# The first image's small key maps in another buffer, and softmax sums inverted in transposed form, in a three-stage attention and expert kernel

## The chip, the cores and the metric

The kernel runs on one core of one Trainium2 chip, as one launch. The metric is the device time of that launch in microseconds (us), the median of three runs. All data are float32.

## What is computed

The input is a batch of 8 images of 256 channels by 32 x 32 pixels. Layer 0 normalises them, attends with pooled keys and values and adds the result back; layer 1 is a self-attention over the 1024 pixels and then a gated mixture of 8 experts. Cut to what the change touches, layer 0 is:

```python
q = einsum('bchw,oc->bohw', x, q_w)                 # 8 heads of 32
k_map, v_map = split(einsum('bchw,oc->bohw', x, kv_w))
def pooled(t):
    outs = []
    for i, r in enumerate([1, 2, 3, 6]):            # maps of 32x32, 16x16, 11x11, 5x5
        p = average_pool(t, r)
        p = p + depthwise_3x3(p, dconv_w[i], dconv_b[i])
        outs.append(p.reshape(B, C, -1))
    return concatenate(outs, axis=2)                # 1426 keys
k, v = layernorm(pooled(k_map)), layernorm(pooled(v_map))
out = softmax(q @ k.T * SCALE) @ v
x = x + proj(mix(out))
```

## The kernel before, in words

**Stages.** Layer 0 and layer 1's attention are woven into one stretch; the experts follow. The last result of layer 0's attention leaves PSUM at 1856.7 us in the profile, the first expert matmul starts at 1893.2 us. What can still be late at the end is TensorE's expert work alone.

**Layer 0's attention** (`attention`, from line 913; main loop from line 1892). Each of the 8 images is worked in 4 units: two groups of four heads (`c`) by two halves of the 1024 pixels. A unit has 11 steps, one for each 128 keys (`kc`); the first unit of an image has one more, `kc` 11, which makes the tail of 18 keys for all four units and is placed ninth, after `kc` 7 (`order`, line 1892). A step makes scores on TensorE (`sc`), takes their exponential on ScalarE into a `pt` buffer of 128 x 2048 (six of them), and one step later multiplies by the values on TensorE (`pv`). The tail's exponentials go to a buffer of their own, `ptail`, of 128 x 4 x 512. There is one PSUM buffer for the scores, so each `sc` waits for the exponential before it.

**Sums.** The `pt` buffers of two steps are added by a DMA that GpSimd's queue issues (`add`, line 1564), and these pairs by VectorE (`sums`, line 1571). A TensorE product with ones gives the sum of each softmax row, 32 equal rows for each head. ScalarE copies this from PSUM to `rec` and in passing records a bound (`hi`); `normalise` (line 1590) inverts `rec` on VectorE, multiplies the unit's output by it, and ScalarE reads `rec` once more for the other bound (`lo`). If a bound is passed, a second, general program runs at the end; it doesn't in this case.

**Keys and values.** A thread projects each image to four maps of 1426 columns (`m` 0 and 1 keys, 2 and 3 values) on TensorE; ScalarE copies each to `p` and writes the middle tap into `acc`. The 3 x 3 convolution is then eight multiply-adds on VectorE for each of the four levels of a map (`taps`, line 1243). For the first image alone, the keys' large level is convolved on TensorE instead (`first_keys`, line 1220), and the keys' `p` lies in two of the six `pt` buffers (`first_maps`, line 1172); their `acc` are the buffers `kn` and `v`. `first_taps` (line 1257) does the values' large level, and then the three small levels of maps 2, 3, 0, 1 in that order. The keys of 1024 to 1425 can be finished once `whole` holds 0 and 1 (`key_tokens`), the values of these columns once it holds 2 and 3 (`value_tokens`).

**What orders the work.** The program is straight-line code for each engine. `Flow` (line 657) writes it: generators (threads) with ranks offer their next instruction, and a table of costs (`cost`, line 723) keeps a planned time for each engine and tile, by which `step` chooses the next thread. Between two steps of the main loop TensorE gets filler work: the projections of the next image, layer 1's weights (`weights1`), layer 1's attention. Everything that a thread issues between two `yield`s is put into the queues as it stands. Every engine then runs its queue in order. `f.finish` in the main loop holds back the next step until a condition is met, and issues what is needed for it first: line 1909 for the keys, line 1921 for the tail, and these lines for the two borrowed buffers:

```python
if i == 4:
    f.finish(lambda: {0, 1}.issubset(whole))
```

All instructions issued through `Flow` carry line 670 in the profile, so its lines are told apart by the names of the tiles.

Of the kernel before, what the change touches and what calls it, by code (L numbers as in the profile page):

```python
# [10 lines left out]
AF = mybir.ActivationFunctionType  # L11
# [5 lines left out]
P = 128  # L17
C = 256
HW = 1024
# [893 lines left out]
def attention(tc, kit, f, outer, ended, nb, consts, x, t1, t2, hn, bounds, vecs, q_t, kv_t, proj_t, gqk_t, wqk, wqkv, vecs1, w1_d, w1c, gate_d, wrc, vecs2, bnvec):  # L913
# [6 lines left out]
    with ExitStack() as ctx:  # L920
# [5 lines left out]
        def T(pool, shape, tag, bufs=1):  # L926
            return f.tile(pool, shape, tag, bufs=bufs)
# [153 lines left out]

        ks, qs, vts = {}, {}, {}
        ptail = T(work, [P, 4, 512], "ptail")
        vz = [T(work, [P, P], f"vz{i}") for i in range(2)]
        for t in vz:
            f.pool.memset(t, 0.0)
# [7 lines left out]
        def ve(*tiles):  # L1094
            return "DVE", tiles, None
# [76 lines left out]
        def first_maps(xp):  # L1172


            for m in range(4):
                if m < 2:
                    p = T(work, [P, 4, 512], "pt", bufs=6).rearrange("p j q -> p (j q)")
                    acc = T(l1, [P, NK], "v") if m else T(work, [P, NK], "kn", bufs=3)
                else:
                    p = pmaps[m - 2]  # L1180
                    acc = T(work, [P, NK], "acc", bufs=3)
                for t in (p, acc):
                    if t is not p or m < 2:
                        f.split(t, 512, HW)
                first[m] = p, acc
            for m, s0 in [(m, s0) for g in (0, 2) for s0 in (0, 512) for m in (g, g + 1)] + [(m, HW) for m in range(4)]:
                if s0 == HW:
                    yield until(lambda: pooled)
                w = min(512, NK - s0)
                c = m % 2  # L1190
                p, acc = first[m]
                src = source(xp, s0, w)
                yield pe(src, tag="sm")
                ps = small()
                for k in range(2):
                    f.pe.matmul(
                        ps[:, :w],
                        lhsT=kvw[:, k, m * P : (m + 1) * P],
                        rhs=src[:, k, :],
                        start=k == 0,  # L1200
                        stop=k == 1,
                    )
                f.act.activation(p[:, s0 : s0 + w], ps[:, :w], AF.Copy)
                for s, n in enumerate(SIDES):
                    a, z = max(OFFS[s], s0), min(OFFS[s] + n * n, s0 + w)
                    if a < z and (m >= 2 or s):
                        f.act.activation(
                            acc[:, a:z],
                            ps[:, a - s0 : z - s0],
                            AF.Identity,  # L1210
                            bias=db(c, s),
                            scale=mid[:, c * 4 + s : c * 4 + s + 1],
                        )
                if (m, s0) == (3, 512):
                    large.append("maps")
                    f.spawn(first_keys(0), 1)
                    f.spawn(first_keys(1), 5)
            whole.append("maps")
# [21 lines left out]
                f.act.activation(acc[:, half * 512 : half * 512 + 512], ps, AF.Identity, bias=db(m, 0))  # L1240
            large.append(("keys", half))

        def taps(c, s, p, acc):
            n, o = SIDES[s], OFFS[s]
            pin = p[:, o : o + n * n].rearrange("p (h w) -> p h w", h=n)
            pout = acc[:, o : o + n * n].rearrange("p (h w) -> p h w", h=n)
            for tap in range(9):
                if tap == 4:
                    continue
                dy, dx, y0, y1, x0, x1 = windows(tap, n)  # L1250
                o_ap = pout[:, y0:y1, x0:x1]
                yield ve(pin[:, y0 + dy : y1 + dy, x0 + dx : x1 + dx], o_ap)
                f.ve.scalar_tensor_tensor(
                    o_ap, pin[:, y0 + dy : y1 + dy, x0 + dx : x1 + dx], dw(c, s, tap), o_ap, ALU.mult, ALU.add
                )

        def first_taps():
            for m in (2, 3):
                yield until(lambda: "maps" in large)
                yield from taps(m - 2, 0, *first[m])  # L1260
                large.append(("values", m))
                read[0] += 1
            yield until(lambda: whole)
            for m in (2, 3, 0, 1):
                for s in range(1, 4):
                    yield from taps(m % 2, s, *first[m])
                whole.append(m)
            done.extend(first[m][1] for m in (2, 3, 0, 1))

# [301 lines left out]
        def sums(n, pairs):  # L1571

            for i in range(1, NKC // 2):
                yield until(lambda: len(pairs) > i)
                for j in range(0, 4, 2):
                    s = pairs[0][:, j : j + 2, :]
                    yield ve(s, pairs[i])
                    f.ve.tensor_tensor(s, s, pairs[i][:, j : j + 2, :], ALU.add)
            yield until(lambda: normalised[0] == n)
            yield pe(pairs[0], tag="sm")  # L1580
            total = small()
            for j in range(4):
                f.pe.matmul(
                    total[DH * j : DH * j + DH, :], lhsT=kit.ones[:, :DH], rhs=pairs[0][:, j, :], start=True, stop=True
                )
            rec = T(work, [P, 512], "rec")
            f.act.activation(rec, total, AF.Copy, accum_out=hi[:, column[n] : column[n] + 1])
            return rec

        def normalise(b, c, sl, rec, n):  # L1590
            att = atts[b, c][:, sl]
            yield ve(rec)
            f.ve.reciprocal(rec, rec)
            f.ve.tensor_tensor(att, att, rec, ALU.mult)
            yield act(rec)
            f.act.activation(rec, rec, AF.Copy, accum_out=lo[:, column[n] : column[n] + 1])
# [276 lines left out]
        mt = T(wp, [P, 2, C], "mt")  # L1873
        bias = T(wp, [P, 2], "mtb")
        def unit(b, c, sl, n, pairs):
            rec = yield from sums(n, pairs)
            yield from normalise(b, c, sl, rec, n)
            normalised[0] += 1
            if c and sl.start:
                f.spawn(project(b), 1)  # L1880
# [23 lines left out]
        for i in range(len(steps) + 1):  # L1904
            if i < len(steps):
                b, c, half, kc = steps[i]
                sl = slice(half * 512, half * 512 + 512)
                if kc % 4 == 0:
                    f.finish(lambda: key_parts[0] > 3 * b + kc // 4)
                if (half, kc) == (0, 0):  # L1910
                    f.finish(lambda: (b, c) in qs and (b or (c, 0) in asked))
                    turn[0] = 2 * b + c
                    atts[b, c] = T(work, [P, HW], "att", bufs=2)
                if kc == NKC // 2 and b < nb - 1:
                    f.sp.dma_start(t1[b][:, c, sl], x[b, c * P : (c + 1) * P, sl])
                if i == 4:
                    f.finish(lambda: {0, 1}.issubset(whole))
                if b == 0 and kc == 0:
                    f.finish(lambda: (c, half) in asked)
                if kc == NKC - 1:  # L1920
                    f.finish(lambda: key_parts[0] > 3 * b + 2 and (b, 1) in qs and (b or len(asked) == 4))
                    tail_scores(b)
                else:
                    pts[i] = scores(b, c, sl, kc)
                f.step()
            if i and steps[i - 1][3] < NKC - 1:
                b1, c1, half1, kc1 = steps[i - 1]
                if kc1 == 0:
                    pv = T(psum, [P, 512], "pv")
                    pairs = []  # L1930
                    sl1 = slice(half1 * 512, half1 * 512 + 512)
                    f.spawn(unit(b1, c1, sl1, units, pairs), 0)
                    units += 1
                f.finish(lambda: kc1 // 4 in vts[b1])
                values(b1, c1, kc1, pts[i - 1], pv)
                if kc1 % 2:
                    add(kc1, pts.pop(i - 1), pts[i - 2])
                    pairs.append(pts.pop(i - 2))
                if kc1 == NKC - 2:
                    u = 2 * c1 + half1  # L1940
                    tail_values(b1, u, pv)
                    pairs.append(pts.pop(i - 1))
                    tail_add(u, pairs[-1])
                    f.finish(lambda: projected[0] >= b1)
                    f.act.activation(atts[b1, c1][:, sl1], pv, AF.Copy)
            if i < len(steps):
                f.step((PACE, PACE1))
# [687 lines left out]
```

## Time and profile before

| what | value |
|---|---|
| runs | 3240.96, 3236.12, 3240.89 us; median 3240.89 us |
| profiled execution | 3236.82 us, of which the span of the instructions is 3235.0 us |
| TensorE busy | 3064.9 us (95%) |
| VectorE busy | 2458.7 us (76%) |
| ScalarE busy | 1692.2 us (52%) |
| GpSimd busy | 1198.6 us (37%) |
| 80.88 to 1860.12 us: TensorE, VectorE, ScalarE busy | 1650.55, 1434.52, 1154.57 of 1779.24 us |
| inversion of a unit's sums on VectorE | 32 times 3.35 us |

The profile is of one execution. In its lines PE is TensorE, PEld its weight load, DVE VectorE, ACT ScalarE, POOL GpSimd, SP SyncE; `out<-in` names what is written and read. In a timeline line the first number is the start in us, the second the length, and the bracket tells how long the engine stood idle before and what ended that.

### The profile page before, as it was taken

Reading aid. Unit: us, or ns where it says so; the run is one execution under the profiler, and the core shown is the slowest. Engines: PE = TensorE matmul, PEld = TensorE weight load, DVE = VectorE, ACT = ScalarE, POOL = GpSimd, SP = SyncE. Lnnn points to the kernel's source line nnn. Section 1 sums busy time; section 2 is a strip of 40 time slices with the busy share of each in tenths; the row PEclk is TensorE's granted clock in tenths of the full one; section 3 lists DMA queues with packets and bytes.
Section 4 is the critical chain, followed back from the end, with each engine's and each line's share of the span. In section 5 each row is a group of like instructions: output and inputs, shape, how many; then the busy total and the mean of one; then the engine's idle time right before and its main releaser. Section 6 shows DMA issues by size and latency. Waiting matters only on the chain.

```text
span 3235.0 us, 55827 instructions
## 1 busy us (share of the span) xinstructions
PE 3064.9 (95%) x22342; PEld 1793.5 (55%) x22342; DVE 2458.7 (76%) x4064; ACT 1692.2 (52%) x2302; POOL 1198.6 (37%) x1293
## 2 busy tenths in 40 slices
PE   8787899999999999989999999999999999999998
PEld 3422234334334334333433367777888888888887
DVE  5787787987898889988754546346888788777776
ACT  3476676576657666676665523334333333444443
POOL 2312314214232232241111210006756666777775
PEclk9799999999999999999999999999999999999999
DMA  1277656665665565764676653124444442000000
GB/s 51 72 157 169 133 115 146 142 138 122 132 152 121 128 144 120 172 144 88 152 161 128 154 205 134 55 90 163 150 143 150 150 163 72 20 30 23 20 14 21
DMA packets 117196, 375.49 MB, mean 116 GB/s; under 512 B 14512, under 2 KB 40440, under 8 KB 93696
## 3 DMA queue, kind: packets, MB, share of 16 engines
q0 software_dynamic: 28608, 179.85, 28.7%
q1 hardware_dynamic: 84960, 190.01, 17.3%
q8 instruction: 178, 2.92, 0.4%
q10 hardware_dynamic: 3360, 1.97, 0.2%
q14 instruction: 90, 0.74, 0.1%
HBM read 118.74 MB, written 87.60 MB: 64 GB/s over the span
## 4 chain that ended last, share of the span: by engine, by line
PE 71%; DVE 10%; ACT 7%; DMA 4%; issue 4%; POOL 2%; ACTq 0%; DVEq 0%; POOLq 0%; SPq 0%
PE bank L670 22%; PE sm L670 17%; PE y L670 10%; PE sc L670 8%; PE sx L670 8%; PE pv L670 6%; ACT pt L670 5%; DMA pt<-pt 3%; DVE acc L670 3%; DVE rec L670 1%; DVE pt L670 1%; DVE h L670 1%; DMA pt<-ptail 1%; DVE c L670 1%; DVE u L670 1%
## 5 line engine op out<-in xcount | busy, mean ns | idle before, releaser
L670 ACT ACTIVATE pt<-sc 128x2048 f32<-128x2048 f32 x352 | 660.7, 1877 | 269.3 <-PE sc L670 226.8
L670 DVE SCALAR_TENSOR_TENSOR acc<-p,vec,acc 128x961 f32<-128x961 f32 (+3 forms) x960 | 554.9, 586 | 32.0 <-ACT acc L670 6.4
L670 PE MATMUL sc<-q,kn 32*128 32x512 f32 (+1 forms) x3072 | 417.3, 644 | 102.0 <-ACT pt L670 97.9
L670 DVE TENSOR_TENSOR pt<-pt,pt 128x1024 f32<-128x1024 f32 x320 | 388.1, 1260 | 125.6 <-DMA pt<-pt 110.4
L670 PE MATMUL pv<-pt,vt 128*32 128x512 f32 x2816 | 380.1, 612 | 0.1
L670 ACT ACTIVATE p1c<-bank 128x256 f32<-128x256 f32 x226 | 86.6, 383 | 556.2 <-PE bank L670 550.2
L670 ACT ACTIVATE h<-h,bnvec 128x512 f32<-128x512 f32 x452 | 341.9, 805 | 62.7 <-DVE h L670 52.6
L670 POOL DMA_DIRECT2D pt<-pt x160 | 146.1, 913 | 561.2 <-ACT pt L670 438.5
L670 POOL TENSOR_TENSOR rstd<-rstd,mhalf 128x4 f32<-128x4 f32 (+2 forms) x88 | 107.5, 1222 | 624.1 <-DVE rstd L670 592.4
L670 DVE TENSOR_TENSOR h<-p1c,bank 128x512 f32<-128x512 f32 x226 | 154.1, 682 | 222.9 <-PE bank L670 216.0
L670 PEld LDWEIGHTS sc<-q,kn 32*128 32x128 f32 (+1 forms) x3072 | 113.6, 178 | 293.4 <-ACT pt L670 195.8
L670 POOL TENSOR_TENSOR tm<-h,tm 128x256 f32<-128x256 f32 x202 | 234.7, 1162 | 15.8
L670 DVE TENSOR_TENSOR h<-u,bank 128x256 f32<-128x256 f32 x452 | 230.2, 550 | 7.8
L670 PEld LDWEIGHTS pv<-pt,vt 128*32 128x32 f32 x2816 | 55.6, 108 | 271.8 <-issue 257.1
L670 PE MATMUL bank<-h,w2e 128*128 128x256 f32 (+1 forms) x620 | 203.6, 457 | 2.8 <-DVE h L670 1.9
L670 POOL TENSOR_TENSOR tm<-h 128x512 f32<-128x512 f32 x101 | 131.8, 1304 | 189.6 <-ACT h L670 189.6
L670 DVE TENSOR_TENSOR h<-h,gate 128x1024 f32<-128x1024 f32 x128 | 199.6, 1560 | 0.5 <-ACT h L670 0.5
L670 PE MATMUL y<-t,s3e 128*128 128x256 f32 x768 | 187.0, 379 | 1.9 <-POOL t L670 1.7
L670 PE MATMUL bank<-t,s1e 128*128 128x256 f32 x750 | 182.5, 379 | 0.2 <-DVE h L670 0.2
L670 POOL TENSOR_TENSOR t<-h 128x512 f32<-128x512 f32 x104 | 135.0, 1298 | 110.3 <-DVE h L670 93.3
L670 PE MATMUL sm<-y,t 128*32 128x256 f32 (+1 forms) x1976 | 175.6, 379 | 0.1
L670 DVE TENSOR_TENSOR u<-h,bank 128x512 f32<-128x512 f32 x226 | 155.5, 688 | 24.7 <-DVE h L670 0.9
(315 smaller groups left out, 5551.8 us busy)
## 6 DMA issues: line engine op xcount, KB each, us to landing
pt<-pt POOLq DMA_DIRECT2D x160, 1024.0 KB, 7.8
h<-h SPq DMA_DIRECT2D x142, 512.0 KB
xi<-in_x_dram SPq DMA_DIRECT2D x16, 512.0 KB
t<-t SPq DMA_DIRECT2D x8, 1024.0 KB
res<-t SPq DMA_DIRECT2D x32, 256.0 KB
t<-res SPq DMA_DIRECT2D x32, 256.0 KB
hn<-res SPq DMA_DIRECT2D x32, 256.0 KB
hn<-hn SPq DMA_DIRECT2D x16, 512.0 KB
```

The costliest lines, as they stand in the source:

```text
L670: ins = fn(*args, **kwargs)
```

## The change

The small levels (columns 1024 to 1425) of the first image's two key maps are copied to `ptail` instead of the borrowed `pt` buffers. `ptail` is first needed for the exponentials of the tail at the ninth step. The borrowed buffers then hold only the large level, which TensorE reads. The small levels are convolved in the order 0, 1, 2, 3, keys first, and the two lines at step 4 are gone. `f.split` lets the planner see the two keys' parts of `ptail` apart.

The sums are inverted otherwise. VectorE transposes the sums within blocks of 32 x 32 from PSUM into `rec`. As the 32 rows of a head are equal, one column of 32 then holds all that is in a block: 16 columns are inverted (128 x 16 in place of 128 x 512), spread to 32 equal columns and transposed back into `rec`. ScalarE's copy for the bound `hi` now writes the sums onto themselves in PSUM, and is issued behind the first transposition, which must have read them.

```diff
         ptail = T(work, [P, 4, 512], "ptail")
+        f.split(ptail, 512)
...
-                f.act.activation(p[:, s0 : s0 + w], ps[:, :w], AF.Copy)
+                small_levels = s0 == HW and m < 2
+                f.act.activation(ptail[:, m, :w] if small_levels else p[:, s0 : s0 + w], ps[:, :w], AF.Copy)
...
-        def taps(c, s, p, acc):
+        def taps(c, s, p, acc, base=0):
             n, o = SIDES[s], OFFS[s]
-            pin = p[:, o : o + n * n].rearrange("p (h w) -> p h w", h=n)
+            pin = p[:, o - base : o - base + n * n].rearrange("p (h w) -> p h w", h=n)
...
-            for m in (2, 3, 0, 1):
+            for m in (0, 1, 2, 3):
+                p, acc = first[m]
                 for s in range(1, 4):
-                    yield from taps(m % 2, s, *first[m])
+                    yield from taps(m % 2, s, *((ptail[:, m, :], acc, HW) if m < 2 else (p, acc)))
                 whole.append(m)
...
                     total[DH * j : DH * j + DH, :], lhsT=kit.ones[:, :DH], rhs=pairs[0][:, j, :], start=True, stop=True
                 )
+            return total
+
+        def normalise(b, c, sl, total, n):
+            att = atts[b, c][:, sl]
             rec = T(work, [P, 512], "rec")
-            f.act.activation(rec, total, AF.Copy, accum_out=hi[:, column[n] : column[n] + 1])
-            return rec
-
-        def normalise(b, c, sl, rec, n):
-            att = atts[b, c][:, sl]
-            yield ve(rec)
-            f.ve.reciprocal(rec, rec)
+            turned = rec.rearrange("p (j i) -> p j i", i=DH)
+            yield ve(total)
+            f.ve.transpose(rec, total)
+            f.act.activation(total, total, AF.Copy, accum_out=hi[:, column[n] : column[n] + 1])
+            one = T(work, [P, 16, 1], "one")
+            f.ve.reciprocal(one, turned[:, :, 0:1])
+            f.ve.transpose(turned, one.to_broadcast([P, 16, DH]))
             f.ve.tensor_tensor(att, att, rec, ALU.mult)
             yield act(rec)
             f.act.activation(rec, rec, AF.Copy, accum_out=lo[:, column[n] : column[n] + 1])
...
-                if i == 4:
-                    f.finish(lambda: {0, 1}.issubset(whole))
```

More of the change, by code (lines that the diff above doesn't have):

```diff
@@ L1875, in unit @@
         def unit(b, c, sl, n, pairs):
-            rec = yield from sums(n, pairs)
-            yield from normalise(b, c, sl, rec, n)
+            total = yield from sums(n, pairs)
+            yield from normalise(b, c, sl, total, n)
             normalised[0] += 1
```

## The prediction

> **What bounds the kernel now.** I read the page's busy line first, then TensorE's waits, then windows of 10 us over the first image, the timeline where the scores stop, and the tile `rec`.
>
> ```profile
> PE 3064.9 (95%) x22342; PEld 1793.5 (55%) x22342; DVE 2458.7 (76%) x4064; ACT 1692.2 (52%) x2302; POOL 1198.6 (37%) x1293
> ```
>
> TensorE is the bound: of the span of 3235.0 us only 170.1 us can come back from its idle time. The windows for 1860 to 3235 us show 1349.1 of 1375 us busy: the experts leave nothing, so a gain must come from layer 0's stretch, and one made there shifts all that follows. In that stretch the largest idle is in the first image (columns: stretch, length, busy us of PE, PEld, DVE, ACT, POOL, clock, DMA share, GB/s):
>
> ```profile
> 100.00:110.00 10.00, 6.17 (x11) 2.62 (x11) 8.95 (x25) 1.79 (x6) 4.01 (x7) 0.66 0.07 14
> 110.00:120.00 10.00, 4.97 (x17) 3.86 (x18) 6.60 (x25) 3.48 (x7) 0.00 (x0) 0.75 0.36 117
> 120.00:130.00 10.00, 6.95 (x24) 5.56 (x22) 8.00 (x27) 0.60 (x1) 0.00 (x0) 0.67 0.00 0
> 130.00:140.00 10.00, 7.22 (x24) 5.93 (x24) 3.92 (x18) 1.37 (x3) 6.70 (x4) 0.73 0.12 39
> 140.00:150.00 10.00, 8.69 (x44) 4.27 (x44) 6.11 (x22) 4.08 (x7) 0.19 (x1) 0.83 0.80 199
> ```
>
> In these 50 us PE is idle for 16.0 us, at a clock of 0.73 on average, and VectorE for 16.4 us. The timeline shows why: no scores are issued between these two lines, while VectorE convolves the small levels, the keys' last.
>
> ```profile
> 94.05 1.35 PE L670 MATMUL sc<-q,kn 32*128 32x512 f32 x8
> ...
> 139.88 5.30 DVE L670 SCALAR_TENSOR_TENSOR v<-pt,vec,v 128x225 f32<-128x225 f32 x17
> ...
> 144.02 1.96 PE L670 MATMUL sc<-q,kn 32*128 32x512 f32 x8
> ```
>
> From 200 to 1890 us PE's waits are nearly all of one kind, and ScalarE stands behind VectorE's inversions at times (columns: total, times, longest):
>
> ```profile
> PE sc L670 <- ACT pt L670: 91.2, 94, 3.3
> ```
>
> ```profile
> ACT pt L670 <- PE sc L670: 218.8, 232, 3.6
> ...
> ACT rec L670 <- DVE att L670: 16.5, 13, 3.2
> ```
>
> ```profile
> L670 DVE RECIPROCAL rec<-rec x32: 3328/3352/3355, 198.3 to 1872.1; 128x512 f32<-128x512 f32 x32
> L670 DVE TENSOR_TENSOR att<-att,rec x32: 691/692/1182, 201.6 to 1875.5; 128x512 f32<-128x512 f32 x32
> ```
>
> One case in order of time: ScalarE's second reading of `rec` waits 3.18 us for VectorE, the exponential behind it waits too, and TensorE waits 2.31 us for that:
>
> ```profile
> 900.39 3.34 DVE L670 RECIPROCAL rec<-rec 128x512 f32<-128x512 f32 x1
> ...
> 904.49 0.63 ACT L670 ACTIVATE rec<-rec 128x512 f32<-128x512 f32 x1 [3.18 <-DVE att L670]
> ...
> 905.11 1.86 ACT L670 ACTIVATE pt<-sc 128x2048 f32<-128x2048 f32 x1
> ...
> 907.02 2.09 PE L670 MATMUL sc<-q,kn 32*128 32x512 f32 x8 [2.31 <-ACT pt L670]
> ```
>
> **What the Trainium skill says.** "VectorE: DVE Perf Modes", section "First, the fixed hardware budget": the reciprocal is an iterated division. The trace agrees that it is dear: 3.35 us against 0.69 us for a product of the same 512 columns. The same page, "The three transpose paths": VectorE transposes 32 x 32 blocks only, at 311 ns for 128 x 128 in bf16; the trace before has no such instruction. "TensorE: Matmul & The Clock Gate", "What's actually happening": an idle array falls to half clock. The trace agrees: four products of 512 columns took 3.62 us from 104.42 us on (0.90 each), eighteen took 7.42 us from 59.83 us on (0.41 each).
>
> **Part 1: ptail, order and the condition gone.** *ScalarE's copies* are the same in number and size: nothing. *Buffers:* `ptail` is first written by exponentials at the ninth step, which needs the keys' third part, so after the taps that read it; no new wait. *Order:* step 4's scores no longer wait for 96 small taps. In the build, the scores of steps 4 to 7, the tail's and two more now stand ahead of the values' third part. Then `pv` of the tenth step waits for the values' small levels, which are now last. So the stall becomes shorter and VectorE sets it.
>
> VectorE, worked from durations before. The values' 48 small taps ended at 103.4 us; now the keys' 48 stand there. The groups `kn` and `v` (24 each) took 8.2 us each, so the values' will take 16.4 us. Before 103.4 us nothing moves. After it, in the new order: four value taps (1.8), five reductions, BN statistics of the keys and their small steps to `tshift` at about 112.5 us. Then `mix` (1.1), three pair additions that were formerly later (3 x 2.35 = 7.1), the other 44 taps (15), `mix` and `weights1` copies (6.7), and two waits for GpSimd's powers for `bnvec` (3.05 us each, less a tap beside each: 5.5). Sum: 36, so the last value tap ends near 148.5 us. Before, the last tap ended at 145.2 us, but without the additions. Add the values' statistics (2.2), one wait for `rstd` (1.0) and the next image's first eight large taps (10.0): 161.7 us. Before, VectorE had three additions and these eight taps behind it at 170.2 us (167.90 + 2.36; the ninth tap begins at 170.18). **The lead is 8.5 us.** It agrees with TensorE: values third part ready at 155.5 us, then about 20.7 us of listed products to the first unit's end, 176 against 185.4 us before, less 1.9 us for one `res` product set that the new order leaves for later: 7.5.
>
> Bounds: nothing, if the additions wait for their DMAs (7.65 to 11.7 us in the chain of waits elsewhere), and 16 us, all of PE's idle time. I take 8.5. By weighing both builds' TensorE order with sizes, as much filler stands ahead of each unit's end in both, so the lead isn't eaten by work drawn forward. *Queues:* on SP the x copy of step 6 moves ahead of layer 1's weight loads (1.54 us of issue, waiting for nothing), and the four `vz` copies, which wait for the values' third part, move from ahead of these loads to behind the third `res` load; the fourth `res` load waits there to about 156 us, and only filler waits for it: nothing either way. On GpSimd three DMAs of pair additions (0.9 us each) now stand ahead of the two `bnvec` powers, which are asked for later than that (about 138 us): nothing, or 2.7 us if they wait for their exponentials.
>
> **Part 2: sums in transposed form, 32 units.** VectorE gives up 3.35 and takes a transposition from PSUM, a reciprocal of 16 columns (the 128 x 2 one took 0.17) and one back. No row has a transposition: the nearest, a 128 x 512 copy from PSUM, took 0.69; the skill's 311 ns times four gives an upper end of 1.25. I take 0.69: 3.35 - 0.69 - 0.17 - 0.69 = 1.80 us a unit, 58 us in all; at 1.25 it is 0.68, 22 us. VectorE isn't the bound (81% busy from 80.88 to 1860.12 us), so most of this is hidden. What reaches PE:
>
> - Second ScalarE wait: from sum to product took a copy (0.6 + 0.19), 3.35 and 0.69; now 0.69 + 0.17 + 0.69 + 0.69, 2.6 us shorter. It takes about 15 of the 16.5 us. In the case above 1.3 of 3.18 us reached PE beyond the usual gap of 1.0, four tenths: **-6 us**.
> - New wait: ScalarE's first copy now stands behind the first transposition, 0.69 us, and behind whatever VectorE does before. In the timeline the reciprocal began 0.12 us after that copy in 20 units, and 0.6 to 3.3 us after it in 12 (22 us in sum). So ScalarE stands 32 x 0.69 + 22 = 44 us, at most; behind it waits the next exponential, and behind that PE's `sc`. But an exponential waited for its scores 232 times, 0.94 us on average, which covers 0.69 in the 20 punctual units. The other 12 exceed it by (22 + 8)/12 - 0.94 = 1.6 us, 19 in all, four tenths of it 7.5, and the planner knows of the wait and sets the copy later: half, **+4 us**. Ends: 0 and 44. The PSUM bank is held as much longer, one of three; fillers have two others: nothing.
> - Relief of a backlog on VectorE's taps: a twentieth of 58: **-3 us**; ends 0 and 20, since 11 inversions of 3.3 us lie in the listed chain and each gets 1.8 us shorter.
>
> **Sum** against the profiled execution: 3236.8 - 8.5 - 6 + 4 - 3 = 3223.3 us. The median is 4.1 us above that execution; the sum from the median would be 3227.4. I take the middle, **3225 us**.
>
> **Rivals.**
> - *ScalarE's new wait decides (slower).* Against: half the units are punctual. For: taps are offered to VectorE up to 4 us ahead, and no `yield` stands before the copy. A share s of the 44 us reaches PE: the end moves by 44s - 17.5. From s = 0.4 on nothing is won, from 0.55 it is slower by over 0.2%; at 0.8: 3241 + 18, about 3257 us.
> - *The lead is lost.* The next image's taps, or DMAs of pair additions, take the 8.5 us back; 3225 + 8.5 = 3234 us. For: VectorE stays at 9.5 of 10 busy us from 190 to 240 us.
> - *VectorE's relief counts in full.* 3225 - 20 + 3 = 3208 us. For: inversions lie in the chain.
> - *The transposition is slow*, 1.25 us: the second wait shrinks by 1.5 instead of 2.6, ScalarE waits 0.56 us longer for 32 units (+4): 3225 + 7, about 3232 us.
>
> **How the numbers follow.** Forecast 0.42, relief 0.20, lead lost 0.17, ScalarE's wait 0.13, slow transposition 0.08. The range 3203 to 3247 us takes in all but the slow rival and a tail of the relief. Faster by over 0.2% (below 3234.4 us; 0.2% is about what a measurement can tell from no change): 0.71, from the forecast, relief and half of the two near 3233; within: 0.16; slower: 0.13.
>
> **What would show it.** Step 4's `sc` near 100 us rather than 144; the tail's near 117; the next long gap of `pv` ends near 155; first `att<-pv` near 177 rather than 185.4. Transpositions of 0.69 us, the lines `ACT rec <- DVE att` nearly gone, and ScalarE's waits for the first transposition well below 44 us. I am wrong if `PE sc <- ACT pt` grows past 91 us, or if the first unit's lead is no longer there at 1856.7 us, the last `att<-pv`.

## The result and the profile after

The changed kernel took **3238.17 us** (median of 12 runs, 3232.11 to 3244.34) against 3240.9 us (12 runs, 3236.12 to 3246.19): ratio 0.9995, 95% interval 0.9986 to 1.0004. The forecast of 3225 us is missed by 13 us; the time lies between before and the forecast, and no difference from before is measured. The profiled execution has a span of 3239.2 us.

First the page's busy line of the changed kernel.

```profile
PE 3072.6 (95%) x22678; PEld 1788.4 (55%) x22678; DVE 2403.2 (74%) x4128; ACT 1690.1 (52%) x2302; POOL 1201.7 (37%) x1293
```

VectorE lost 55.5 us of work (58 forecast), and TensorE gained nothing: 166.6 us idle instead of 170.1, and 7.7 us longer busy. The windows over the first image (columns as in the prediction: PE, PEld, DVE, ACT, POOL, clock, DMA share, GB/s):

```profile
100.00:110.00 10.00, 8.06 (x60) 2.38 (x56) 9.58 (x26) 5.41 (x8) 3.99 (x7) 0.83 0.53 107
110.00:120.00 10.00, 8.30 (x84) 2.97 (x82) 9.62 (x27) 8.29 (x11) 2.27 (x3) 1.00 0.71 144
120.00:130.00 10.00, 6.76 (x96) 2.70 (x64) 9.06 (x25) 5.64 (x3) 0.00 (x0) 1.00 0.50 102
130.00:140.00 10.00, 8.53 (x58) 6.72 (x59) 6.47 (x23) 1.09 (x3) 2.92 (x1) 0.73 0.00 0
140.00:150.00 10.00, 6.75 (x28) 4.65 (x26) 6.43 (x28) 4.16 (x10) 3.23 (x3) 0.93 0.21 52
```

Where TensorE was idle for 16.0 us of these 50 it is now idle for 11.6, at a mean clock of 0.90 instead of 0.73. The timeline shows the scores of step 4 at 98.47 us and the tail's (32 x 32) at 119.48; the old hole from 95 to 144 us is closed.

```profile
98.47 1.14 PE L670 MATMUL sc<-q,kn 32*128 32x512 f32 x8 [0.25 <-ACT kn L670]
103.72 1.93 PE L670 MATMUL sc<-q,kn 32*128 32x512 f32 x8
...
119.48 1.14 PE L670 MATMUL sc<-q,kn 32*32 32x512 f32 x32
```

How much that brings the first unit is seen in the group of `att<-pv` (shortest/median/longest ns, then the first and the last start), before and after:

```profile
L670 ACT ACTIVATE att<-pv x32: 578/597/602, 185.4 to 1856.7; 128x512 f32<-128x512 f32 x32
```

```profile
L670 ACT ACTIVATE att<-pv x32: 588/597/610, 172.7 to 1870.1; 128x512 f32<-128x512 f32 x32
```

The first unit ends 12.7 us earlier (8.5 forecast). The last ends 13.4 us later, as if something between had taken the lead back. The length of the inversion isn't it; the groups by shape (busy time, mean ns | idle time before them) have its three new instructions (seven more first transpositions read `sx` instead of `sm`):

```profile
L670 DVE STREAM_TRANSPOSE rec<-one 128x512 f32<-128x512 f32 x32 | 22.8, 711 | 1.1
L670 DVE STREAM_TRANSPOSE rec<-sm 128x512 f32<-128x512 f32 x25 | 17.8, 712 | 14.4 <-PE sm L670 14.4
L670 DVE RECIPROCAL one<-rec 128x16 f32<-128x16 f32 x32 | 8.1, 253 | 1.1
```

That is 0.71 + 0.25 + 0.71 = 1.67 us in place of 3.35. ScalarE's groups of the same view show the price:

```profile
L670 ACT ACTIVATE rec<-rec 128x512 f32<-128x512 f32 x32 | 20.1, 629 | 11.9 <-DVE att L670 11.7
L670 ACT ACTIVATE sm<-sm 128x512 f32<-128x512 f32 x25 | 14.6, 582 | 46.1 <-DVE rec L670 46.0
...
L670 ACT ACTIVATE sx<-sx 128x512 f32<-128x512 f32 x7 | 4.1, 584 | 7.2 <-DVE rec L670 7.1
```

The copies for `hi` stand **53.1 us** (46.0 + 7.1) behind the first transposition; the prediction's outer bound was 44. The second reading still waits 11.7 us instead of 16.5. One case in the timeline:

```profile
389.74 1.95 DVE L670 SCALAR_TENSOR_TENSOR acc<-p,vec,acc 128x240 f32<-128x240 f32 x4
...
391.61 0.71 DVE L670 STREAM_TRANSPOSE rec<-sm 128x512 f32<-128x512 f32 x1
392.36 0.58 ACT L670 ACTIVATE sm<-sm 128x512 f32<-128x512 f32 x1 [3.82 <-DVE rec L670]
...
392.94 1.87 ACT L670 ACTIVATE pt<-sc 128x2048 f32<-128x2048 f32 x1
...
394.86 2.09 PE L670 MATMUL sc<-q,kn 32*128 32x512 f32 x8 [3.55 <-ACT pt L670]
```

VectorE is still at taps of the next image when the sums are ready, so the transposition starts late. ScalarE stands 3.82 us in its queue, the exponential behind the copy comes as late, and TensorE has nothing for 3.55 us. Then it is slow as well: these eight products take 2.09 us at a granted clock of 0.50, the eight at 98.47 us took 1.14 (clock 1.00 from 98 to 99 us). That an idle array falls to half clock is in the Trainium skill, "TensorE: Matmul & The Clock Gate", "What's actually happening", and the trace agrees; here a stop of 3.55 us costs some 0.95 us more in the products behind it. Such stretches count as busy time.

In sum, from 200 to 1890 us, TensorE's waits for exponentials are fewer and longer than before (columns: total, times, longest; before 91.2, 94, 3.3):

```profile
PE sc L670 <- ACT pt L670: 83.3, 67, 6.5
```

### The profile page after: what moved, and what is told of

The parts are those of the page before. It is cut to its first block, busy times and chain, and to the rows that moved or that the text cites. A ratio compares the mean times of both kernels' runs of the same rounds, so it can differ in the third digit from the quotient of the medians.

```text
span 3239.2 us, 56567 instructions
## 1 busy us (share of the span) xinstructions
PE 3072.6 (95%) x22678; PEld 1788.4 (55%) x22678; DVE 2403.2 (74%) x4128; ACT 1690.1 (52%) x2302; POOL 1201.7 (37%) x1293
## 2 busy tenths in 40 slices
DMA packets 117200, 375.54 MB, mean 116 GB/s; under 512 B 14512, under 2 KB 40440, under 8 KB 93696
## 5 line engine op out<-in xcount | busy, mean ns | idle before, releaser
L670 PE MATMUL sc<-q,kn 32*128 32x512 f32 (+1 forms) x3072 | 424.1, 653 | 98.5 <-ACT pt L670 94.8
L670 PE MATMUL pv<-pt,vt 128*32 128x512 f32 x2816 | 388.8, 625 | 2.8 <-ACT vt L670 2.8
L670 PE MATMUL sm<-p,v 128*32 128x256 f32 (+1 forms) x2424 | 199.8, 379 | 0.0
```

What stands on the lines that cost most here:

```text
L670: ins = fn(*args, **kwargs)
```

## The experiments

Three theories, which the expectations name by letter or in words. **W**: the new wait of ScalarE took the gain. **S**: the lead of the first image is lost on the way, for want of filler or of `pt` buffers. **P**: the planner lays every edit's queues out anew, and the order alone scatters the time by as much. Ratios are to before, with runs of before on the same chip, and the brackets behind them are 95% intervals; one thousandth is 3.2 us.

### The two parts alone

Part 1 alone: the changed kernel with the old inversion.

```diff
-            f.ve.transpose(rec, total)
...
+            f.act.activation(rec, total, AF.Copy, accum_out=hi[:, column[n] : column[n] + 1])
...
+            f.ve.reciprocal(rec, rec)
```

> The kernel before with part 1 alone: ptail for the keys' small levels, keys first, the condition at step 4 gone; the sums are inverted as before. Theory W (part 2's new wait of ScalarE behind the first transposition eats part 1's lead): part 1 alone keeps the lead of the first unit (12.7 us in the profile of the changed kernel) to the end, 3229 to 3233 us against 3241 before. Theory S (the lead is given back in image 1, where TensorE has no filler and the scores run against pt buffers that wait for their additions): 3237 to 3242 us, no measurable change; the first att<-pv near 173 us and the lead in TensorE work under 3 us by 300 us. Theory P (every edit reshuffles the planned order, and that scatter is as large as either part): nothing is foretold beyond 3241 plus or minus 10.

Measured: 3286.1 us, ratio 1.0138 (1.0122 to 1.0154). Part 2 alone: the kernel before with the new inversion and nothing of `ptail`.

> The kernel before with part 2 alone: sums transposed, 16 columns inverted, transposed back, ScalarE's first copy behind the first transposition. Theory W: slower than before, 3244 to 3255 us, with ScalarE waits on the tile rec of 85 to 100 us between 200 and 1890 us (74 before, layer 1's among them). Theory S: about 3238 us. Theory P: 3241 plus or minus 10.

Measured: 3274.52 us, ratio 1.0107 (1.0092 to 1.0123).

Each part alone is slower, by 45 and 35 us, outside what any of the three theories expected, and both together are not. No sum of effects of the parts explains this. In part 1 alone other instructions moved with it: its DMAs carry 388.10 MB against 375.49.

### The order alone

The kernel before, with one cost in the planner's table changed by 1.5%. The same work is done; only the queues are laid out differently.

```diff
         if op == "reciprocal":
-            return 0.1 + 0.0064 * n
+            return 0.1 + 0.0063 * n
```

> The kernel before, same instructions, but the planner's cost for the unit's reciprocal is 3.33 us instead of 3.38 (3.35 measured): only the order changes. Theory P (scatter of the planned order): off 3240 us by 5 us or more, to either side, up to 40. Against P: within 3 us of 3240.

Measured: 3271.23 us, ratio **1.0101** (1.0084 to 1.0119). Its waits from 200 to 1890 us, where TensorE's was 91.2 us before:

```profile
PE sc L670 <- ACT pt L670: 107.1, 93, 4.0
...
DVE rec L670 <- ACT rec L670: 36.8, 16, 4.2
```

Part 1 alone with the same change of cost, and the changed kernel with its transpositions planned at 0.71 instead of 0.70 us:

> Part 1 alone with the reciprocal planned at 3.33 us instead of 3.38. If part 1 itself costs 45 us (a wait or a queue that it makes worse): 3275 to 3295 us again. If the 45 us are the order's luck, theory P: well below 3275, and with the first unit's lead kept as low as 3229.

> The changed kernel with the transpositions planned at 0.71 us (what the trace shows) instead of 0.70. Theory P: off 3238 us by 5 us or more to either side. Theory W has no reason for a change: 3235 to 3241.

Measured: 3248.6 us (1.003, 1.0019 to 1.004) and 3248.54 us (1.0024, 1.0015 to 1.0034). Two more of the kind: part 2 alone with its transpositions planned at 0.71, and the kernel before with 0.15 in place of 0.1 in the line above:

> Part 2 alone, with the transpositions planned at 0.71 instead of 0.70 us, so that only the order of the queues is another than in the first run of part 2 alone (3274.5 us). If the order is what that run lost by, this one lies elsewhere by 10 us or more, anywhere from 3235 to 3285 us. If part 2 itself costs it (its wait on ScalarE), it is 3270 to 3279 us again.

> The kernel before with its reciprocal planned at 0.05 us more instead of less, so again only the order is another. If the order before is a good draw out of a scatter, this one is slower too, by 5 to 45 us: 3245 to 3285 us. If the first change of this kind (3271 us) was a freak, 3237 to 3244 us.

Measured: 3294.57 us (1.017, 1.015 to 1.0191) and 3275.79 us (1.0106, 1.0085 to 1.0127). For part 2 alone both ranges of the expectation were missed. In three of these five the work changed a little with the order: the DMAs carry 388.08 MB instead of 373.42 in part 2 alone, 375.55 instead of 388.10 in part 1 alone, 369.25 instead of 375.49 in the last run, and a few instructions differ (VectorE 4066 for 4064, GpSimd 1305 for 1293 in the last). In the first run of the kernel before (375.50 MB) and in that of the changed kernel (375.54) the bytes and the instruction counts of VectorE, ScalarE and GpSimd stay what they were, within 0.01 MB, so these two show the order alone.

**P holds**: a change of a few hundredths of a microsecond in one planned cost moves the kernel before by 33 and 34 us, part 1 alone by 35, part 2 alone by 20, the changed kernel by 9 (by the ratios). Order alone accounts for the first 33 and the last 9. The single parts say nothing about their worth; what can be compared has to have the same order.

### The new inversion in the order of before

So the next kernel keeps every queue of before. (In its trace all of TensorE's 22342 products come in the order of before; with the changed cost above some 3800 of them stood elsewhere. In the runs below that keep the changed kernel's order at most 2 of 22678 do.) The planner is told that the new inversion costs what the old did; ScalarE's copy, in place in PSUM, stays ahead of the first transposition. It is part 2 without its new wait.

```diff
+        if op == "transpose":
+            return 0.0064 * (512 - 16) if ins[0].space == PSUM else 0.0
...
-            f.act.activation(rec, total, AF.Copy, accum_out=hi[:, column[n] : column[n] + 1])
+            f.act.activation(total, total[:, 0:512], AF.Copy, accum_out=hi[:, column[n] : column[n] + 1])
...
-            f.ve.reciprocal(rec, rec)
+            f.ve.transpose(rec, total)
+            f.ve.reciprocal(one, turned[:, :, 0:1])
+            f.ve.transpose(turned, one.to_broadcast([P, 16, DH]))
```

> The kernel before with the inversion in transposed form, but every engine's queue in the order of before: the planner is told that the three instructions cost what the one reciprocal did, and ScalarE's first copy stays where it was, ahead of the first transposition (it writes the sums onto themselves in PSUM), which waits for it. So this is the shorter inversion alone, 1.7 us in 32 places, without the new wait and without another order. If VectorE's relief reaches TensorE, as the prediction had it (second wait 6, backlog 3): 3230 to 3234 us. If VectorE's inversions lie in the chain in full: about 3221 us. If neither: 3239 to 3242 us.

Measured: 3237.04 us (22 runs), ratio 0.9989 (0.9981 to 0.9997): **3.6 us** better (1 to 6). ScalarE's second reading in this kernel:

```profile
L670 ACT ACTIVATE rec<-rec 128x512 f32<-128x512 f32 x32 | 20.0, 624 | 0.8 <-DVE att L670 0.8
```

Its waits are gone (0.8 of 16.5 us), as the prediction worked out, but 15.7 us less waiting and 51 us less work on VectorE bring only 3.6 us.

### The changed kernel without its new wait

The order of the changed kernel is kept; where the copy of the sums stands, ScalarE copies 128 columns of constants, which waits for nothing. Layer 0's bound `hi` is left out. `f.note` puts the new copy into the queue and lets the planner count the old one.

```diff
-            f.act.activation(total, total, AF.Copy, accum_out=hi[:, column[n] : column[n] + 1])
+            ins = nc.scalar.activation(junk, ident, AF.Copy)
+            f.note("ACT", "activation", ins, (total, total, AF.Copy), {"accum_out": hi[:, column[n] : column[n] + 1]})
```

> The changed kernel, every queue in its order, but in place of ScalarE's copy of the sums stands a copy of 128 constant columns to a scratch tile, 0.2 us shorter, which waits for nothing: the bound hi of layer 0 is not recorded. Theory W: the gaps of TensorE behind this copy (391, 623, 1413, 1591 and 1842 us in the profile, 15.6 us in sum) go, and 3238 becomes 3220 to 3226 us. Theory S or P: at most a third of it, 3233 to 3238 us.

Measured: **3226.03 us**, ratio 0.9957 (0.9944 to 0.997), 12.3 us below the changed kernel by the ratios, with both intervals some 5 us to either side. Of the five gaps that the expectation names, those near 391, 623 and 1591 us (9.9 us in sum) are gone; those near 1413 and 1842 us stay. This copy is 0.30 us long instead of 0.58 and 0.19, so a second run makes three such copies, 0.92 us together:

> The run without the new wait again, in the changed kernel's order of queues (the bound of layer 0 isn't recorded), but in place of the copy of the sums ScalarE makes three copies of 128 columns of constants, 0.90 us together, so that it works as long as in the changed kernel (0.58 and 0.19 us) and only doesn't wait. If the 12 us were the wait, it ends as the run without the new wait, near 3226 us. If they were the shorter copy (some 0.5 us for 32 units, 15 us of ScalarE), it ends near 3238 us.

Measured: 3229.65 us, ratio 0.997 (0.9958 to 0.9982). The two groups of these copies:

```profile
L1610 ACT ACTIVATE junk<-con 128x128 f32<-128x128 f32 x64 | 19.6, 306 | 1.0
L1611 ACT ACTIVATE junk<-con 128x128 f32<-128x128 f32 x32 | 9.9, 310 | 1.0
```

They stood 2.0 us where the copy stood 53.1. With ScalarE working slightly longer than in the changed kernel, the wait alone is worth **8 us** (ratios 0.9995 and 0.997; 3 to 13 us with both intervals); the 4 us between the two runs come from the shorter copy, if they are real. **W holds.** Of the 51 us that ScalarE no longer stood, about a sixth reached the end. The copy also holds its PSUM bank longer. That stopped TensorE just once between 200 and 1890 us, for 1.66 us at 1362 us, so most of the price must come by what stands behind the copy in ScalarE's queue.

### The copy ahead of the transposition, planned anew

The changed kernel with ScalarE's copy in place ahead of the first transposition, which then waits for it.

> The changed kernel with ScalarE's copy for the bound issued ahead of the first transposition, in place in PSUM, as the kernel before had it; the transposition waits for the copy. Theory W: ScalarE's waits on the tile rec fall by about 40 us, and the time lies near that without the wait (3226 us) plus some scatter: 3220 to 3235 us. Theory P: the order is another, so anything from 3225 to 3280 us, and only the waits, not the time, follow W.

```diff
+            f.act.activation(total, total, AF.Copy, accum_out=hi[:, column[n] : column[n] + 1])
             return total
...
             f.ve.transpose(rec, total)
-            f.act.activation(total, total, AF.Copy, accum_out=hi[:, column[n] : column[n] + 1])
```

Measured: 3236.46 us, ratio 0.9994 (0.9984 to 1.0005), as the changed kernel. ScalarE's wait at the copy falls from 53.1 to 3.9 us, but that of the second reading grows from 11.7 to 27.6. The order is another one here: gaps of 3.9 and 4.0 us at 1131.7 and 1159.1 us stand behind exponentials that wait over 4 us for DMA additions. Inconclusive by itself.

### Is a lead in the first image carried to the end?

By the falling back of the last `att<-pv` to 1870.1 us the lead seemed lost, as S says. The test takes the lead away and leaves every queue as it was: 15 reciprocals of 128 constants ahead of the small levels of the values (in the changed kernel) or of the keys (in the kernel before). `f.hold` puts an instruction into a queue without the planner counting it.

```diff
+                if m == 2:
+                    for _ in range(15):
+                        f.hold("DVE", nc.vector.reciprocal(idle, idle))
                 for s in range(1, 4):
```

> The changed kernel in its own order of queues, with 15 reciprocals of 128 constants (some 13 us of VectorE in all, unknown to the planner) put ahead of the values' small levels of the first image, so that the lead of 12.7 us that the first unit had is taken away and nothing else is changed. If a lead that is made in the first image is carried to the end (the step of the prediction), the end moves by the whole of it: about 3251 us. If in this order the lead is worth nothing, since the waits later than it are set by other things (buffers, additions by DMA, filler that has run out), it stays within 4 us of the changed kernel: 3238 to 3242 us. A share in between says what part is carried.

> The kernel before in its own order, with the same 15 reciprocals ahead of the keys' small levels, so that step 4's scores and the first unit come some 13 us later. If a shift in the first image passes to the end, 3240 + 13, about 3253 us. If it is absorbed in later idle time or later filler, under 3244 us. This says whether the sentence that a gain made there shifts all that follows holds in the order of before.

Measured: 3256.46 us, ratio 1.0044 (1.0029 to 1.0058), against 0.9995: **15.9 us** more than the changed kernel. And 3254.65 us, ratio 1.0043 (1.0028 to 1.0058): **13.9 us** more than before. Either difference is known to some 5 us. The hold itself, in the changed kernel's order (durations, then the first and the last start), with the group of `att<-pv`:

```profile
L1283 DVE RECIPROCAL idle<-idle x15: 944/953/955, 103.8 to 117.6; 128x128 f32<-128x128 f32 x15
...
L670 ACT ACTIVATE att<-pv x32: 590/597/631, 189.5 to 1888.6; 128x512 f32<-128x512 f32 x32
```

15 x 0.953 = 14.3 us. The first unit is 16.8 us later than without the hold (189.5 - 172.7), the last 18.5. In the order of before the two are 13.9 and 19.0:

```profile
L670 ACT ACTIVATE att<-pv x32: 578/597/602, 199.3 to 1875.7; 128x512 f32<-128x512 f32 x32
```

**S falls.** In a fixed order the delay at 110 us reached the end in full, as far as 5 us can tell, in both kernels: nothing later made up for it. For the changed order this is the worth of its lead; in the order of before only a delay was tried, no lead. The last `att<-pv` was a bad gauge of the lead. In the run without the new wait it is at the time of before, 1856.6 us for 1856.7, though that kernel's profiled execution is 8.6 us shorter: from there to the end it is 1369.8 us in that kernel and 1378.3 us before, so some 8.5 us of work lie ahead of it in one order and behind it in the other.

```profile
L670 ACT ACTIVATE att<-pv x32: 588/597/606, 172.8 to 1856.6; 128x512 f32<-128x512 f32 x32
```

### The bounds from 16 columns

A version without the wait that still records both bounds. VectorE sums the 16 columns that it inverts, and the 16 inverted ones; ScalarE's two passes are no longer issued (with `f.planned` the planner still counts them, so the order is the changed kernel's). A bound is then a sum over 16 columns a row instead of 512; as the 32 rows of a head hold different columns after the transposition, every sum is still in one of them.

```diff
-            f.act.activation(total, total, AF.Copy, accum_out=hi[:, column[n] : column[n] + 1])
+            f.planned("ACT", "activation", (total, total, AF.Copy), {"accum_out": hi[:, column[n] : column[n] + 1]})
+            f.hold("DVE", nc.vector.tensor_reduce(hi[:, column[n] : column[n] + 1], turned[:, :, 0], AX.X, ALU.add))
...
+            f.hold("DVE", nc.vector.tensor_reduce(lo[:, column[n] : column[n] + 1], one[:, :, 0], AX.X, ALU.add))
...
-            f.act.activation(rec, rec, AF.Copy, accum_out=lo[:, column[n] : column[n] + 1])
+            f.planned("ACT", "activation", (rec, rec, AF.Copy), {"accum_out": lo[:, column[n] : column[n] + 1]})
```

> The changed kernel in its own order, but both bounds of layer 0 are sums over the 16 columns that are inverted (two VectorE reductions of 16 columns a unit), so that ScalarE's copy of the sums and its reading of the inverted sums are no longer issued, although the planner still counts them. If ScalarE's waits behind the inversion cost what the run without the new wait showed, 12 us, and the second reading's 12 us of waits cost some 3 more, it ends near 3223 us; the added reductions cost VectorE some 10 us, of which little reaches the end. If the run without the new wait was faster only because its copy was shorter or left out its reading, this one is the same or faster too; if the wait was not the cause, it stays near 3238 us.

Measured: **3225.54 us** (8 runs), ratio 0.9956 (0.9941 to 0.9971): faster than before and, by the ratios, 12.6 us faster than the changed kernel. Taking away the second reading too brought nothing measurable over the run without the new wait.

### Part 1 alone in the changed kernel's order

The old inversion in the places of the new: copy to `rec`, reciprocal of 512 columns, while the planner counts the new one.

```diff
-            f.ve.transpose(rec, total)
-            f.act.activation(total, total, AF.Copy, accum_out=hi[:, column[n] : column[n] + 1])
+            f.hold("ACT", nc.scalar.activation(rec, total, AF.Copy, accum_out=hi[:, column[n] : column[n] + 1]))
...
+            f.hold("DVE", nc.vector.reciprocal(rec, rec))
```

> Part 1 alone, but every queue in the order that the changed kernel has (the planner counts the new inversion, while the old one is issued: ScalarE's copy to rec at the same place of its queue, then the reciprocal of 512 columns in the place of the transposition). Nothing is left out. If the terms add up in a fixed order, it is the changed kernel without the new wait (8 to 12 us less) and without VectorE's relief (some 3.5 us more), or before less the lead of 12.7 us: 3228 to 3234 us. If part 1 itself costs what its own build showed, it ends near 3286 us; then the order isn't the cause.

Measured: 3270.47 us, ratio 1.0093 (1.0076 to 1.0109). **The expectation failed by 36 us**: the terms don't add up across orders. The group and one case in ScalarE's timeline show where:

```profile
L670 ACT ACTIVATE rec<-rec 128x512 f32<-128x512 f32 x32 | 20.1, 628 | 57.1 <-DVE att L670 57.0
```

```profile
325.40 0.58 ACT L1604 ACTIVATE rec<-sm 128x512 f32<-128x512 f32 x1
325.88 0.20 ACT L1604 ACTIVATION_READ_ACCUMULATOR rec<-sm 128x1 f32 x1
330.22 0.63 ACT L670 ACTIVATE rec<-rec 128x512 f32<-128x512 f32 x1 [4.14 <-DVE att L670]
```

The order was laid out for an inversion planned at 1.6 us, and in 10 of the 32 units the second reading stands directly behind the first (in the order of before in none). With 3.35 us between them ScalarE stands 57.0 us at the second reading instead of 11.7, 41 of them in these ten units, and TensorE gets gaps of 5.0 us (at 326.5) and 5.2 us (at 1873.3). The first unit's lead is untouched (172.4 us). By the ratios this run is 32 us above the changed kernel, so a wait of ScalarE may cost far more than the sixth found above; how the 32 us divide wasn't separated. So this run doesn't give part 1's own worth. It shows that an order depends on the durations that it was planned with.

## Why the prediction was wrong

Its mechanisms were there; the sizes of the new wait and of the relief failed, the lead was sized too small, and one cause was missing.

- **Lead, -8.5: right, and too small.** The first unit came 12.7 us earlier (bounds 0 and 16), and the holds show that this is carried: 13.9 and 15.9 us at the end for 14.3. VectorE's part of the sum was right, the last small tap of the values ended at 147.5 us (148.5 forecast); TensorE's next `pv` came at 151.7 us, where their third part was expected ready only at 155.5. "One made there shifts all that follows" stands. The rival "the lead is lost" falls.
- **Inversion: right.** Predicted 0.69 + 0.17 + 0.69 us, measured 0.71 + 0.25 + 0.71. The skill's 311 ns for 128 x 128 in bf16 ("VectorE: DVE Perf Modes", "The three transpose paths") gave an estimate of 1.25 us as the upper end; here 128 x 512 in f32 took 0.71, so that end and its rival fall.
- **Second wait, -6, and relief, -3: too large.** In the order of before both together are 3.6 us (1 to 6), though the waits do vanish (0.8 of 16.5 us). "Four tenths" was read off one gap at 900 us; even if all 3.6 us were the waits', it would be 0.23 of 15.7. The rival that the relief counts in full falls. In the changed order 11.7 us of waits are left, 10.9 of them in the ten units whose second reading stands directly behind the copy.
- **New wait, +4: the step that failed.** It was "half" of 7.5 us, because "the planner knows of the wait and sets the copy later" and because exponentials that wait for their scores cover 0.69 us. The planner did not make the wait smaller: where 12 late units were reckoned with, with 30 us of waiting, 17 units waited longer than 0.8 us, up to 4.9, and these make 46 us. The wait was 53.1 us in all, past the bound of 44, and 8 to 12 us of it reached the end. Not halved, at 7.5, the term would have lain in what was measured. The PSUM bank, put at nothing, is at most the one stop of 1.66 us. The rival of this wait had the mechanism right, but its shares were too large: it asked for 0.4 of 44 us to undo the gain; with some 0.2 of 53 a large part of the gain was undone.
- **Missing: the order.** The prediction took the two orders for equal but for the steps that it named. One planned cost, changed by 1.5%, moves before by 33 us. The range of 3203 to 3247 held the result, but neither of its ends came from this; that it did is partly luck, since the changed kernel planned with 0.71 instead of 0.70 us took 3248.5. "As much filler stands ahead of each unit's end in both" doesn't hold at the last unit, by some 8.5 us.
- **Its signs of being wrong.** `PE sc <- ACT pt` did not grow past 91 us (83.3). The last `att<-pv` did lose the lead, but it was a bad gauge. The sign that counted was ScalarE's wait for the first transposition, expected well below 44 us.
- **Slips that change nothing.** The items of the sum of 36 us add up to 35.4; 3241 + 18 is 3259, not 3257; of the eighteen products, sixteen had 496 columns.

By measured terms: -12.7 (lead), -3.6 (inversion), +8 to +12 (wait) give -8 to -4 us; measured are -1.6 by the ratio, with an interval of -4.5 to +1.3. The terms come from two orders and are known to 3 to 5 us each, and part 1 in the changed order shows how far such a sum may be off, so the 3 to 7 us between are left to the order and to noise; they were not separated. The forecast's own terms add up to -13.5. Of the 12 us from there to -1.6, 4 to 8 are the wait and 5.4 the relief, 4.2 the other way the lead, and 3 to 7 stay open. The thirteenth is the forecast's starting point, a middle between the profiled execution and the median.

Open stay: what in an order decides its time (three orders of the kernel before lie up to 34 us apart), and what part 1 would be worth alone in an order planned well for it. The new wait put into the order of before wasn't tried: the copy must be issued behind the transposition, which moves its place in the queue.

## What to carry to other kernels

Before an edit of a kernel with a planned order is priced or its parts are tried alone, let the order change with no work changed: take that spread as the least width of the forecast. Then measure each term with the queues held as they are; a delay put in on purpose tells in one run whether a gain at that place would reach the end. And an instruction that only records something doesn't belong on a queue that feeds the bound engine, behind another engine's work: here it stood 53 us, and a sum over 16 columns on the engine that has them gave a bound as well, for 12 us less.

## What the runs showed of the hardware

- VectorE's transposition within 32 x 32 blocks takes 0.71 us for 128 x 512 in f32, from PSUM and from a broadcast source of 16 columns alike; a copy of that size from PSUM took 0.69.
- A reciprocal took 0.25 us for 16 columns, 0.95 for 128, 1.75 for 256 and 3.35 for 512.
- After a stop of 3.55 us eight score products took 2.09 us instead of 1.14, at a granted clock of 0.50 instead of 1.00.
